# Attention preparation in four pieces of two PSUM banks, and a changed order of late work, in a two-layer attention and expert kernel

## The chip, the cores and the metric

The kernel runs on one core of a Trainium2 chip. The metric is device time of one execution in microseconds (us), the median of the runs shown. Five engines work from queues of their own: PE (matrix products), DVE (vector work), ACT (activation functions and copies), POOL (general work) and SP, which here only issues DMAs. Each works through its queue in the order in which the program was written, and an instruction at the head of a queue that waits holds everything behind it. The kernel schedules by hand: the order in the Python text is the order on the engines.

## The reference

The input x is 32 x 128 x 256, that is 4096 tokens of 256 channels in fp32.

```python
# layer 0: attention over all 4096 tokens, 8 heads of 32, causal in t = position % 128
x1 = (h - mu) / sqrt(var + 1e-5) * ln_g + ln_b
q  = (x1 @ wq.T + bq + sym_emb) @ wQ.T + bQ          # two products, folded into one matrix
K, V = h @ wK.T + bK, h @ wV.T + bV
attn = softmax(where(mask, -inf, Q K^T / sqrt(32)));  ctx = attn V
x = h + alpha * (ctx @ out_w.T + out_b)
# layer 1: windowed attention (24 wide), then a dense mixture of 8 experts
t = t + window_attention(ln(t))
w = softmax(ln(t) @ Wr + br)                          # per token, 8 shares
t = t + sum_e w_e * (relu(bn(relu(bn(ln(t) W1_e)) W2_e)) Wo_e + bo_e)
```

## The kernel before

**Layer 0.** The queries are cut into 8 blocks of 512 (`b`), the heads into 2 groups of 4 (`g`). A unit `(b, g)` is a row of steps (`k`), one for each 128 keys that the block may see; a block has 8b+5 steps (6 for b=0), 265 in all. One step is: `scores` (L1299), four heads' score products side by side on the PE, one head into tile `sa` (a pool of one bank), three heads into `sb` (a tile of three banks, from the pool `ps_b` that holds two such tiles); `product` (L1389), the attention-times-V products `av` of the step two before; `exps`, the ACT exponentials of `sa` (L1312) and `sb` (L1314) into one of five `pt` buffers; and `add`, which on DVE adds the `pt` of the step before to the running sum `acc` (L1375, two instructions of 128x1024). On a step that crosses the mask, POOL writes zeros into `pt` (L1326) before anybody reads it. At the end of a unit, ACT copies `av` out between its two exponentials (L1404), the PE sums `acc` over keys (L1419), ACT copies that out (L1447), and SP, DVE and DMA invert and spread it; six and twelve steps later follow `invert` and `scale` (L1471).

Between steps, the loop takes pieces of work from a generator, at an even rate of `count` pieces in a block. `prep(b + 1)` makes the next block's operands in seven pieces: the transposes of x (`pst`, L984), K for the two groups (`psk`, L993), V in two halves (`psv`, L1027), Q for the two groups (`psq`, L1006). Each piece takes a `sb` tile from `ps_b`, uses one bank of it (the transposes two), and gives it back when ACT (K, V) or DVE (Q: a multiplication L1010, then an addition L1014) has read it. So the second step after a piece waits with its three `sb` heads for that reader. Q's readers stand in DVE's queue behind the `add` of the step before. Two more generators follow in blocks 2 and 3: `output_weights` (load, transposes `ps_wo` L1053, copies L1059 and alpha on DVE, then `ps_ob`) and `expert_norms`.

In block 1 the layer-norm statistics of the last tokens are ready, and the roots for blocks 2 to 7 are made at once after that step's piece (`rstd_block(2, NBLK)`: an addition on DVE, a root on ACT, a reciprocal on DVE); the root needs another ACT table than the exponentials. `send_rstd` (L972, L976) then writes the reciprocals to DRAM and reads them back spread over partitions, as `rb`, which Q's multiplication needs.

In block 7 the tokens of the first four blocks are loaded, and on POOL the output bias is added to the first 12 tiles of 128 tokens (`with_bias`, L904; `FIRST` is 12).

**Layer 1.** 64 rounds (`work`: 8 token blocks x 8 experts) of two expert layers, each layer in two halves `first` and `last` of the seven products of a fast 2x2 scheme (`Layer`, L2017), and the weighted output products (`combine`, L2074). Everything else (projection of the next tokens, window attention, routing, biases) is a list of `jobs` with costs and predecessors. `insert` puts up to three jobs at a time between the halves; a job is taken when the planner's clock `now` is `LATER` = 3.2 planner units beyond each predecessor and the share allowed by the block's due times is not used up. Within `last`, ACT makes three `relu`s, of which two wait for a DVE addition (L2059).

Of the kernel before, what the change touches and what calls it, by code (L numbers as in the profile page):

```python
# [823 lines left out]
def fast_kernel(ctx: ExitStack, tc: tile.TileContext, ins: dict, out: bass.AP, narrow):  # L824
# [101 lines left out]
    with ExitStack() as l0:  # L926
# [63 lines left out]

        def project_k(b, g, hT, ps):
            for c in range(2):
                nc.tensor.matmul(  # L993
                    ps, lhsT=wKT[:, c, g * P : (g + 1) * P], rhs=hT[:, c, :],
                    start=(c == 0), stop=(c == 1),
                )
            nc.scalar.activation(
                kT[:, g, b * BLK : (b + 1) * BLK], ps, AF.Identity, bias=colT[:, g, 5:6]
            )

        def project_q(b, g, hT, ps, wait=False):
            if b not in qblk:
                qblk[b] = px.tile([P, NGRP, BLK], F32, tag="q", name=f"q{b}")
            q = qblk[b]
            for c in range(2):
                nc.tensor.matmul(  # L1006
                    ps, lhsT=wcT[:, c, g * P : (g + 1) * P], rhs=hT[:, c, :],
                    start=(c == 0), stop=(c == 1),
                )
            nc.vector.tensor_tensor(q[:, g, :], ps, rblk[b], op=ALU.mult)  # L1010
            qv = q[:, g, :].rearrange("p (t n) -> p t n", n=N)

            def biases():
                nc.vector.tensor_tensor(  # L1014
                    qv, qv, cq[:, g, :].unsqueeze(1).to_broadcast([P, BLK // N, N]), op=ALU.add
                )

            if wait:
                return biases
            biases()  # L1020

        def project_v(b, i2, hT, ps):
            ps = ps.rearrange("p (k d) -> p k d", d=D)
            for k in range(2):
                i = 2 * i2 + k
                for c in range(2):
                    nc.tensor.matmul(  # L1027
                        ps[:, k, :], lhsT=hT[:, c, i * P : (i + 1) * P], rhs=wVT[:, c, :],
                        start=(c == 0), stop=(c == 1),
                    )  # L1030
            j = b * TPB + 2 * i2
            nc.scalar.copy(v[:, j : j + 2, :], ps)

        def prep(b, banks):

            hT = transposed_x(b, banks(f"pst{b}", 2))
            yield
            for g in range(NGRP):
                project_k(b, g, hT, banks(f"psk{b}_{g}", 1)[0])
                yield  # L1040
            for i2 in range(TPB // 2):
                project_v(b, i2, hT, banks(f"psv{b}_{i2}", 1)[0])
                yield
            for g in range(NGRP):
                project_q(b, g, hT, banks(f"psq{b}_{g}", 1)[0])
                yield

# [129 lines left out]
        def output_weights(banks):  # L1177
# [7 lines left out]
            yield  # L1185
            transposed(woT, wo_n, "ps_wo", banks, False)
            nc.vector.tensor_scalar(woT, woT, alpha, None, op0=ALU.mult)
# [51 lines left out]
        with ExitStack() as at:  # L1239
# [267 lines left out]
            load_at = {2: ("xs", 5, 6), 3: ("xs", 7), 5: ("xg", 2), 7: ("xg", 3)}  # L1507

            def rest_of_first():
                for i2 in range(TPB // 2):  # L1510
                    project_v(0, i2, hT0, banks(f"psv0_{i2}", 1)[0])
                    yield
                for g in range(1, NGRP):
                    project_k(0, g, hT0, banks(f"psk0_{g}", 1)[0])
                    yield
                    project_q(0, g, hT0, banks(f"psq0_{g}", 1)[0])
                    yield

            todo, done, count = iter(()), 0, 0
            later = {}  # L1520
            for n in range(len(steps) + LAG + 1 + 16):
                if n < len(steps):
                    b, g, k = steps[n]
                    own = sum(len(units[b, i]) for i in range(NGRP))
                    if g == 0 and k == 0:
                        for _ in todo:
                            pass
                        todo, done, count = iter(()), 0, 7
                        if b + 1 < NBLK:
                            todo = prep(b + 1, banks)  # L1530
                            if not b:
                                send_rstd(1)
                        if b == 0:
                            todo, count = itertools.chain(rest_of_first(), todo), 11
                        if b == 2:
                            todo, count = itertools.chain(todo, output_weights(banks)), 10
                        if b == 3:
                            todo, count = itertools.chain(todo, expert_norms(banks)), 9
                        if 2 <= b < NBLK - 2:
                            xblk[b + 2] = load_x(b + 2, "xg")  # L1540
                    scores(b, g, k)
# [23 lines left out]
                if n < len(steps):  # L1565
                    at_step = g * len(units[b, 0]) + k + 1
                    closing = any(f is close_sums for f, _ in later.get(n, []))
                    while done < count * at_step // own and not (closing and b):
                        next(todo, None)
                        done += 1  # L1570
                    if b == NBLK - 1 and not g and k < 4:
                        load_tokens(
                            k, tok.tile([P, TPB, D], F32, tag="xg", name=f"tokens{k}")
                        )
                    if n in load_at:
                        for lb in load_at[n][1:]:
                            got = xstat if load_at[n][0] == "xs" else xblk
                            got[lb] = load_x(lb, load_at[n][0])
                    for sb_, si in stat_at.get(n, ()):
                        stats(sb_, si, xstat[sb_])  # L1580
                        if (sb_, si) == (NBLK - 1, TPB - 1):
                            rstd_block(2, NBLK)
                            send_rstd(2)
                            nsq = px.tile([P, NTILE], F32, tag="nsq", name="nsq", bufs=1)
                            nc.gpsimd.tensor_tensor(
                                nsq, mean0[:, :, 0], mean0[:, :, 0], op=ALU.mult
                            )
                            nc.gpsimd.tensor_tensor(nsq, nsq, mean0[:, :, 1], op=ALU.add)
                            nc.vector.tensor_reduce(hmax, nsq, axis=AX.X, op=ALU.max)
                    if 1 < b < NBLK - 1 and not g and k == 1:  # L1590
                        send_rstd(b + 1)
                    if b == NBLK - 1 and g and 4 <= k < 4 + FIRST:
                        with_bias(k - 4)
                for f, u in later.pop(n, []):
# [409 lines left out]
    class Layer:  # L2004
# [43 lines left out]
        def last(self):  # L2048
            x, t, w, s, out = self.x, self.t, self.w, self.s, self.out
            if t is None:  # L2050
                self.plain(1)
                return
            self.product(self.a[:, 0], w[:, 1, :P], x[:, 1, :HB], False)
# [7 lines left out]
                self.u.unsqueeze(1).to_broadcast([P, 2, HB]), op=ALU.add,  # L2061
            )
            relu(out[:, 0, HB:], out[:, 0, HB:], self.l, e, 0)
            relu(out[:, 1, :], out[:, 1, :], self.l, e, 1)
# [273 lines left out]
    for b in range(1, NBLK):  # L2338
# [33 lines left out]
        for r2 in range(TPB // 2):  # L2372
# [3 lines left out]
            )  # L2376
        job(("sums", b), 0, lambda b=b: expert_sums(b), ("xfT", b, 0), ("xfT", b, 1))
        job(("route", b), 0.55, lambda b=b: route(b), ("xfT", b, 0), ("xfT", b, 1))
        job(("routet", b), 0.15, lambda b=b: turn_route(b), ("route", b))
        job(("routex", b), 0, lambda b=b: route_exponentials(b), ("routet", b))  # L2380
        job(("routed", b), 0, lambda b=b: route_shares(b), ("routex", b))
        job(("turn_shares", b), 0.2, lambda b=b: turn_shares(b), ("routed", b))
        for r2 in range(TPB // 2):
            job(
                ("bias", b, r2), 0.6, lambda b=b, r2=r2: output_biases(b, r2),
                ("turn_shares", b),
            )
# [26 lines left out]
    now, spent = 0.0, 0.0  # L2414
    LATER = 3.2
    SPAN = E * 9.5
# [24 lines left out]
    def insert(passed):  # L2441
# [4 lines left out]
        while k < len(jobs) and few < 3:  # L2446
            name, cost, f, needs = jobs[k]
            if cost and spent >= allowed():
                k += 1
                continue  # L2450
            if all(done_at.get(q, now) + LATER <= now for q in needs if q in known):
                f()
# [20 lines left out]
    for k in range(len(work)):  # L2473
# [7 lines left out]
        if k + 1 < len(work):  # L2481
# [5 lines left out]
            if not k:  # L2487

                one.last()
            else:  # L2490
                insert(1.73)
        if k >= 2:
            combine_half()
# [4 lines left out]
        if one and k:  # L2498
            one.last()
            insert(1.3)  # L2500
# [3 lines left out]
        if one:  # L2504
            name = f"th{k + 1}"
            h1[k + 1] = one.out, token_sums(one.out, "th", name) if k + 1 >= PLAIN else None
        two.last()
        h2[k] = two.out
        insert(1.3)
    while halves:  # L2510
        combine_half()
# [47 lines left out]
```

## Time and profile before

| what | value |
| --- | --- |
| median of three runs | 1516.95 us (1516.86 to 1518.46) |
| the profiled execution: its own time, its span | 1517.62 us, 1515.8 us |
| busy: PE, DVE, ACT, POOL | 1472.3, 1205.0, 941.3, 166.6 us |
| layer 0, from the first exponential to the end of its scores | 20 to 717 us of the span |
| expert rounds of layer 1 | about 790 to 1506 us |
| mean granted PE clock | 0.995 of full speed |

Spans and busy times are of the one profiled execution. A busy engine isn't an engine at its peak: matrix products that wait for one of their operands part of the time can count as busy. So a stretch is read by the pace of its steps, that is by the distance of the starts of successive exponentials, and not only by busy shares. A wait in the profile is put down to the engine that came last.

### The profile page before, as it was taken

The numbers are of one execution on the slowest core, as the hardware profiler recorded it, in microseconds if no ns is written. First come the engines' busy times: TensorE is split into PE (matmuls) and PEld (weight loads), VectorE is DVE, ScalarE is ACT, GpSimd is POOL, SyncE is SP. The second block draws the span as 40 slices with busy tenths as digits, with TensorE's granted clock in tenths as the row PEclk, the third lists the DMA queues.
The fourth block names the chain that finished last, engine by engine and source line by source line (L and its number), as shares of the span: only waits on it lengthen the run. The fifth ranks groups of instructions, "written<-read, shape, count | busy, mean of one in ns | idle before, by whom it ended". The sixth has DMA issues, their size and how long they took to land.

```text
span 1515.8 us, 23636 instructions
## 1 busy us (share of the span) xinstructions
PE 1472.3 (97%) x8873; PEld 843.4 (56%) x8873; DVE 1205.0 (79%) x2191; ACT 941.3 (62%) x1356; POOL 166.6 (11%) x318
## 2 busy tenths in 40 slices
PE   9999999999999999999899999999999999999998
PEld 5333232222322222222558787887888788788887
DVE  5678789899989898999647777777787777777775
ACT  4777778878878888987353544554355444544443
POOL 2101011100000000071153012100011000000000
PEclk9999999999999999999999999999999999999999
DMA  7120101010000010000333333433333334333342
GB/s 150 26 51 19 36 1 37 2 29 9 3 13 8 1 50 22 1 9 10 108 119 104 105 119 108 135 123 107 118 108 122 104 116 141 106 121 118 126 153 65
DMA packets 96377, 110.15 MB, mean 73 GB/s; under 512 B 17949, under 2 KB 85232, under 8 KB 96256
## 3 DMA queue, kind: packets, MB, share of 16 engines
q1 hardware_dynamic: 93280, 106.87, 23.7%
q8 instruction: 72, 1.18, 0.3%
q0 software_dynamic: 1888, 0.91, 0.3%
q10 hardware_dynamic: 1088, 0.79, 0.2%
q14 instruction: 49, 0.40, 0.1%
HBM read 98.87 MB, written 8.53 MB: 71 GB/s over the span
## 4 chain that ended last, share of the span: by engine, by line
PE 70%; DVE 17%; ACT 6%; issue 5%; DMA 0%; POOL 0%; ACTq 0%; DVEq 0%; POOLq 0%
PE psh L2017 18%; PE sa L1299 13%; PE av L1389 12%; PE psy L2074 11%; DVE acc L1375 6%; ACT h L2000 3%; PE psk L993 2%; PE psv L1027 2%; PE psq L1006 2%; PE sb L1299 2%; PE psk L1766 2%; DVE h L2059 1%; PE sums L1419 1%; ACT pt L1314 1%; DVE tokens L2082 1%
## 5 line engine op out<-in xcount | busy, mean ns | idle before, releaser
L1375 DVE TENSOR_TENSOR acc<-acc,pt 128x1024 f32<-128x1024 f32 (+2 forms) x470 | 523.8, 1178 | 35.7 <-POOL pt L1326 20.9
L1314 ACT ACTIVATE pt<-sb 128x1536 f32<-128x1536 f32 (+1 forms) x265 | 382.8, 1445 | 6.2 <-PE sb L1299 6.1
L1299 PE MATMUL sa<-q,kT 32*128 32x512 f32 (+3 forms) x576 | 297.5, 602 | 8.7 <-ACT pt L1312 5.4
L1299 PE MATMUL sb<-q,kT 32*128 32x512 f32 (+3 forms) x1728 | 301.2, 603 | 3.2 <-DVE woT L1059 1.6
L2000 ACT ACTIVATE h<-h,bshift,bscale 128x256 f32<-128x256 f32 x244 | 159.2, 699 | 222.2 <-DVE h L2059 222.1
L1389 PE MATMUL av<-pt,v 128*32 128x512 f32 (+3 forms) x2304 | 283.1, 571 | 0.5
L2074 PE MATMUL psy<-wo,h 128*128 128x256 f32 x1024 | 242.8, 380 | 0.0
L2074 PEld LDWEIGHTS psy<-wo,h 128*128 128x128 f32 x1024 | 191.8, 190 | 29.1 <-issue 2.9
L1312 ACT ACTIVATE pt<-sa 128x512 f32<-128x512 f32 (+1 forms) x265 | 157.9, 596 | 80.5 <-PE sb L1299 44.2
L1299 PEld LDWEIGHTS sa<-q,kT 32*128 32x128 f32 x576 | 86.3, 184 | 212.6 <-ACT pt L1312 164.3
L1389 PEld LDWEIGHTS av<-pt,v 128*32 128x32 f32 x2304 | 47.9, 108 | 199.4 <-issue 175.0
L2082 DVE SCALAR_TENSOR_TENSOR tokens<-psy,w,tokens 128x256 f32<-128x256 f32 x256 | 111.1, 475 | 35.2 <-PE psy L2074 34.9
L2044 DVE TENSOR_TENSOR u<-psh,u 128x256 f32<-128x256 f32 x122 | 51.2, 419 | 104.8 <-ACT u L2043 104.5
L1326 POOL MEMSET pt<- 32x256 f32 (+4 forms) x123 | 52.1, 424 | 609.3 <-ACT pt L1314 521.9
L2000 ACT ACTIVATE h<-psh,bshift,bscale 128x256 f32<-128x256 f32 (+1 forms) x132 | 75.6, 574 | 46.7 <-PE psh L2017 39.1
L1299 PEld LDWEIGHTS sb<-q,kT 32*128 32x128 f32 x1728 | 90.5, 184 | 14.0 <-ACT pt L1314 6.5
L2043 ACT COPY u<-psh 128x256 f32<-128x256 f32 x122 | 43.9, 360 | 80.3 <-PE psh L2017 79.9
L2017 PE MATMUL psh<-tx,s 128*128 128x256 f32 x366 | 89.9, 382 | 0.3 <-DVE tx L1990 0.3
L2017 PE MATMUL psh<-th,s 128*128 128x256 f32 x366 | 90.2, 383 | 0.0
L2059 DVE TENSOR_TENSOR h<-psh,u 128x512 f32<-128x512 f32 x122 | 83.2, 682 | 4.5 <-PE psh L2017 4.5
L2017 PEld LDWEIGHTS psh<-th,s 128*128 128x128 f32 x366 | 70.3, 192 | 9.9 <-DVE h L2059 0.2
L2017 PEld LDWEIGHTS psh<-tx,s 128*128 128x128 f32 x366 | 69.8, 191 | 10.4 <-DVE tx L1990 0.7
(335 smaller groups left out, 1788.2 us busy)
## 6 DMA issues: line engine op xcount, KB each, us to landing
w<-in_L_ffn_W_dram SPq DMA_DIRECT2D x128, 256.0 KB
s<-kept SPq DMA_DIRECT2D x56, 512.0 KB
wo<-in_L_ffn_Wo_dram SPq DMA_DIRECT2D x64, 256.0 KB
xg<-in_x_dram SPq DMA_DIRECT2D x32, 128.0 KB
tokens<-in_x_dram SPq DMA_DIRECT2D x8, 512.0 KB
kept<-s SPq DMA_DIRECT2D x8, 512.0 KB
out_dram<-tokens SPq DMA_DIRECT2D x32, 128.0 KB
rec<-flat SPq DMA_DIRECT2D x60, 64.0 KB
```

Source lines behind the costliest of these rows:

```text
L1299: nc.tensor.matmul((sb[:, h - 1, :] if h else sa)[:, at : at + w], lhsT=kT[rows, gg, j * P : (j + 1) * P], rhs=q[rows, gg, lo : lo + w], s ...
L1312: nc.scalar.activation(pt[:, 0, used], sa[:, used], AF.Exp, scale=SCALE)
L1314: nc.scalar.activation(pt[:, 1:, used], sb[:, :, used], AF.Exp, scale=SCALE)
L1326: nc.gpsimd.memset(rows, 0.0)
L1375: nc.vector.tensor_tensor(acc[:, hs, cols], acc[:, hs, cols], pt[:, hs, at : at + w], op=ALU.add,)
L1389: nc.tensor.matmul(av[h * HD : (h + 1) * HD, lo : lo + w], lhsT=v[:, j, (g * HG + h) * HD : (g * HG + h + 1) * HD], rhs=pt[:, h, at : at + w],
L2000: nc.scalar.activation(dst, src, AF.Relu, bias=bshift[:, m, k : k + 1], scale=bscale[:, m, k : k + 1])
L2017: nc.tensor.matmul(ps, lhsT=w, rhs=x, start=start, stop=True, skip_group_check=True)
L2044: nc.vector.tensor_tensor(u, a[:, 1], u, op=ALU.add)
L2059: nc.vector.tensor_tensor(flat.rearrange("p (k c) -> p k c", k=2), self.q, self.u.unsqueeze(1).to_broadcast([P, 2, HB]), op=ALU.add,)
L2074: nc.tensor.matmul(ps[:, i, :], lhsT=ht[:, c, r * P : (r + 1) * P], rhs=wo[k][:, c, :], start=(c == 0), stop=(c == 1),)
L2082: nc.vector.scalar_tensor_tensor(out=tokens(n), in0=ps[:, i, :], scalar=w[:, r, e : e + 1], in1=tokens(n), op0=ALU.mult, op1=ALU.add,)
```

## The change

1. `prep` has four pieces: the transposes, both groups of K, both halves of V, both groups of Q. Each of the last three uses two banks of one `ps_b` tile, all its products first and then the two copies (for Q: multiplication and addition of group 0, then of group 1). The rest of block 0's own preparation is done likewise in two pieces. `count` is 5 (8 in blocks 0 and 2, 7 in block 3).
2. `output_weights` takes one tile with two banks for its transposes, and ACT copies them.
3. After the last statistics, only a mark is set. Ahead of the next piece the addition, the root and a reload of the exponentials' table are put in (`root_rstd`), and one step later the reciprocal, `send_rstd(2)` and the rest (`invert_rstd`).
4. The tokens of blocks 0 to 2 are loaded in block 5, those of block 3 in block 6; the 12 `with_bias` run as six in block 5 and six in block 6.
5. In layer 1, `expert_sums` stands behind `route` and `turn_route` in the list; the second half of `output_biases` of a block waits for the first; `LATER` becomes a variable, 3.2 for rounds 0 to 7 and 4.7 from round 8; the two late `relu`s of the second expert layer are issued after the `insert` that follows.

```diff
         def prep(b, banks):
             hT = transposed_x(b, banks(f"pst{b}", 2))
             yield
-            for g in range(NGRP):
-                project_k(b, g, hT, banks(f"psk{b}_{g}", 1)[0])
-                yield
...
+            pss = banks(f"psk{b}", 2)
+            keys = [project_k(b, g, hT, pss[g], True) for g in range(NGRP)]
+            for f in keys:
+                f()
+            yield
...
+            pss = banks(f"psq{b}", 2)
+            queries = [project_q(b, g, hT, pss[g], later=True) for g in range(NGRP)]
+            for f in queries:
+                f()
+            yield
...
-            transposed(woT, wo_n, "ps_wo", banks, False)
+            pss = banks("ps_wo", 2)
...
+            for c in range(2):
+                nc.scalar.copy(woT[:, c, :], pss[c][:, :D])
...
+            def root_rstd():
+                cols = slice(2 * TPB, NTILE)
+                nc.vector.tensor_scalar(
+                    rstd0[:, cols], mean0[:, cols, 1], 1e-5, None, op0=ALU.add
+                )
+                nc.scalar.activation(rstd0[:, cols], rstd0[:, cols], AF.Sqrt)
+                ready(AF.Exp)
+
+            def invert_rstd():
+                cols = slice(2 * TPB, NTILE)
+                nc.vector.reciprocal(rstd0[:, cols], rstd0[:, cols])
+                send_rstd(2)
...
+            u, z = NBLK - 3, NBLK - 2
+            tokens_at = [(u, 0, 2), (u, 0, 4), (u, 1, 0), (z, 1, 0)]
...
-                        todo, done, count = iter(()), 0, 7
+                        todo, done, count = iter(()), 0, 5
...
+                    if due == 2:
+                        invert_rstd()
+                        due = 0
                     while done < count * at_step // own and not (closing and b):
+                        if due == 1:
+                            root_rstd()
+                            due = 2
                         next(todo, None)
                         done += 1
...
-                    if b == NBLK - 1 and g and 4 <= k < 4 + FIRST:
-                        with_bias(k - 4)
+                    if NBLK - 3 <= b < NBLK - 1 and g and 4 <= k < 4 + FIRST // 2:
+                        with_bias((b - NBLK + 3) * FIRST // 2 + k - 4)
...
-        job(("sums", b), 0, lambda b=b: expert_sums(b), ("xfT", b, 0), ("xfT", b, 1))
         job(("route", b), 0.55, lambda b=b: route(b), ("xfT", b, 0), ("xfT", b, 1))
         job(("routet", b), 0.15, lambda b=b: turn_route(b), ("route", b))
+        job(("sums", b), 0, lambda b=b: expert_sums(b), ("xfT", b, 0), ("xfT", b, 1))
...
-                ("turn_shares", b),
+                ("turn_shares", b), *([("bias", b, r2 - 1)] if r2 else []),
...
+        if k == E:
+            later = 4.7
...
-        two.last()
+        relus = two.last()
         h2[k] = two.out
+
         insert(1.3)
+        relus()
```

## The prediction

> **What bounds the kernel now.** I read the page first, then the steps of layer 0 in the timeline, then the waits of the PE.
>
> ```profile
> PE 1472.3 (97%) x8873; PEld 843.4 (56%) x8873; DVE 1205.0 (79%) x2191; ACT 941.3 (62%) x1356; POOL 166.6 (11%) x318
> PE 70%; DVE 17%; ACT 6%; issue 5%; DMA 0%; POOL 0%; ACTq 0%; DVEq 0%; POOLq 0%
> L1375 DVE TENSOR_TENSOR acc<-acc,pt 128x1024 f32<-128x1024 f32 (+2 forms) x470 | 523.8, 1178 | 35.7 <-POOL pt L1326 20.9 <-ACT pt L1314 12.7
> ```
>
> The PE bounds the span, but 17% of the chain that ended last is DVE, nearly all of it `acc` in layer 0. A plain step there takes 2.07 us: score products began at 440.48 and 442.55, and 1.06 + 1.0 us of PE work fill it. ACT needs 0.60 + 1.45 = 2.05. DVE needs more: twenty-one adds took 23.93 us near the end, so one per 1.136 us and 2.27 us a step. DVE falls 0.20 us behind in every plain step and catches up only while the PE does a preparation piece (`psq` 1.91 us). Five `pt` buffers let it fall back by about 6 us (the exponential of step n+5 would start 8.3 us after that of step n ends; the add takes 2.3); then steps take 2.27. Where DVE's backlog meets something that needs DVE at once, the PE loses. Block 5:
>
> ```profile
> 428.85 1.98 PE L1006 MATMUL psq<-hT,wcT 128*128 128x512 f32 x4
> 432.83 1.12 PE L1299 MATMUL sa<-q,kT 32*128 32x512 f32 x2
> 434.02 0.67 DVE L1010 TENSOR_TENSOR q<-psq,rb 128x512 f32<-128x512 f32 x1
> 434.74 1.13 PE L1299 MATMUL sb<-q,kT 32*128 32x512 f32 x6 [0.79 <-DVE q L1010]
> 439.58 0.60 ACT L1312 ACTIVATE pt<-sa 128x512 f32<-128x512 f32 x1 [2.20 <-PE sb L1299]
> ```
>
> Q's products ran at 428.85; DVE read them only at 434.02, after its adds; `sb` of the second next step needs that tile and began at 434.74 instead of with `sa` at 432.83. Exponentials started at 433.99, 439.58 for consecutive `sa` of steps 17 and 18: with the delayed `sb` this pair of steps took 3.5 us more than 2 x 2.07. Two other places, and block 7:
>
> ```profile
> 64.10 1.28 ACT L915 ACT_TABLE_LOAD   x1
> 65.63 1.28 ACT L1312 ACT_TABLE_LOAD   x1
> 154.75 0.75 DVE L1059 COPY woT<-ps_wo 128x256 f32<-128x256 f32 x2
> 155.22 1.44 PE L1299 MATMUL sb<-q,kT 32*128 32x512 f32 x6 [1.57 <-DVE woT L1059]
> 646.17 25.15 POOL L904 TENSOR_TENSOR tokens<-tokens,outb 128x256 f32<-128x256 f32 x11
> 655.63 13.43 DVE L1375 TENSOR_TENSOR acc<-acc,pt 128x1024 f32<-128x1024 f32 x8 [0.64 <-ACT pt L1314]
> ```
>
> Two table loads in front of exponentials; `woT` as Q above; and eight adds in 13.43 us while POOL adds biases, a pitch of 1.67 instead of 1.136. In block 7 DVE is busy without a gap from 655.63 to the end of its adds at 719.8 and so sets the end of layer 0. In layer 1 the PE's named waits between 790 and 1506 us sum to 12.8 us:
>
> ```profile
> PE psa L1831 <- ACT ptl L1822: 2.1, 2, 1.2
> PE ptf L1895 <- DVE xf L1885: 1.7, 2, 0.9
> PE psa L1831 <- DVE tokens L1959: 1.4, 1, 1.4
> PE psp L1819 <- ACT s L1808: 1.4, 1, 1.4
> PE psrt L1920 <- DVE lgT L1915: 1.2, 1, 1.2
> ```
>
> These are jobs whose predecessor on ACT or DVE wasn't done, each under 1.5 us.
>
> **What the Trainium skill says.** "SBUF — State Buffer", Who interferes with whom: a DVE instruction with two SBUF inputs contends with a POOL instruction that reads SBUF, and the second is held up. The trace agrees in kind (adds of 1.22 us take 1.75 beside `with_bias`, and the first bias lasted 9.41 us, until DVE had a gap), though both go on at a lower rate. "ScalarE: Activation LUTs", What ACT_TABLE_LOAD costs: 1283 ns, with a drain beside it; here the two loads are 1.28 us each and the whole episode (64.10 to 66.93) 2.83, so no further drain is seen. The same lines give the price used below.
>
> **The change part by part.**
>
> *Biases out of block 7.* Ten adds in the second half of block 7 were slowed by 1.67 - 1.136 = 0.53 us, 5.3 us, and a later one by 0.45. DVE sets the end there, so -5.6 us. In blocks 5 and 6 they cost DVE at most 12 x 0.53 = 6.4 us. What hides it: DVE is idle there for 8.0 of 114.9 and 8.9 of 127.2 us, POOL can start them only in a DVE gap, and these are at the boundary of the two units and at the V piece just after it. I take 0; without this cover it is +6.4. The three early 512 KB token loads precede reciprocal DMAs on SP, which have five or more steps to spare; nothing.
>
> *Pieces of two banks.* PE, ACT and DVE work is the same: 7 pieces of 1.0 + 6 x 1.91 = 12.5 us a block become 1.0 + 3 x 3.83. K's and V's copies (0.69, 0.58 each) end 0.7 us after the piece; the tile is needed 2.07 after it: no wait. Q: DVE reads group 0, adds its bias, reads group 1: 0.69 x 3 = 2.07 us after it is through with its earlier add, and the tile is needed 3.83 + 2.07 after the piece starts. So there is no loss while DVE is through with that add within 3.83 us of the piece's start; one bank alone allows 1.91 + 2.07 - 0.69 = 3.3. The add ends 1.3 us plus the backlog after the start, so the backlog may be 2.5 rather than 2.0. Losses of this kind before, from the starts of exponentials against steps without such a piece: 3.5 (block 5), 2.0, 1.25 and 3 x 0.4 at block starts (second Q piece as last step of the block: 5.05, 4.29, 3.4 against 3.04), 0.6 and 0.95 in blocks 4 and 6: 9.5 us. Afterwards, by the order of the changed program, Q stands 3 to 11 steps behind V, where DVE has just had 3.8 us to catch up. Backlog at Q: 7 to 9 steps x 0.20 + 0.24 (`invert`) + 0.3 (mask step) = 2.0 to 2.4 in blocks 4 and 5, no loss; 10 steps, and `scale` (1.26) before it, 3.85 in block 6: 1.3 us of wait and some 0.7 since `sa` then runs without `sb`. With 1 us for the rest, 3.0. So -6.5; bounds -9.5 and +3. The last steps of a unit, where the PE had also waited for Q, are relieved, and nothing else stands there.
>
> *Roots.* Before, step 10 came 6.42 us after its predecessor, with a K piece 3.98 expected: 2.4 lost. Afterwards 2 x 1.28 + 0.4 us of ACT work stand beside K's 3.83 us of PE, but K's two copies (1.38) follow them, so the next exponential is about 0.7 late. -1.7. `rb` is due later: the write of 4-byte elements took from 65.98 until the read could issue at 75.14, and SP must first wait for another reciprocal; I get a landing near 85 us and Q's read near 86. If late, +2; so 0 to -2.4.
>
> *Output weights.* Steps 38 and 39 took 6.04 and 3.82; 2 x 2.07 and 1.3 us of PE work leave 4.4 lost. One tile and ACT copies take this away, but now the transposes come one step behind the load instead of three: the load issues behind four DMAs that wait for the unit's sums (in the trace 139.57 to 142.08), and needs 3 to 4 us; the PE arrives about 2.6 us early. With 0.6 for `ps_ob`, -1.2 (0 to -4).
>
> *Block 0.* K now follows the transposes at once and waits for two copies (1.2 us); shorter turns of tiles give as much back: 0.
>
> *Layer 1.* Waiting 1.5 units longer covers waits up to 1.5 us. Of the PE gaps between rounds 8 and 63, about 8.5 us are of this kind; the bias order frees banks (the 1.4 of `psa` on `tokens`); `relu`s behind the jobs' ACT work free ACT, which sat 222 us before them, and their reader comes more than 5 us later. Chains get longer (some 19 links), yet in the changed program each block's transposed tokens stand at least 20 us of expert products before their first use. I take -7, bounds -12 and +2.
>
> Sum: -5.6 - 6.5 - 1.7 - 1.2 - 7 = -22.0. The profiled execution, 1517.6 (span 1515.8), goes to 1495.6; its time is 0.7 above the median, so the median goes from 1516.95 to 1495.
>
> **The rivals.**
> (a) Layer 1 gives nothing: new waits come at other jobs. For: jobs move, and with them their bank turns. Against: every wait in the list is shorter than what is added. 1502.
> (b) Layer 0 gives half: `rb` or `wo_n` late, the biases meeting Q in blocks 5 and 6 (+6.4 on backlogs that stand near the limit). 1503.
> (c) Slower: DVE is at its full backlog of 6 us at every Q piece. It then reads Q 7.3 us after the start, 3.5 too late, with 1.1 for the heads apart: 4.6 x 7 blocks = 32 us, against 25 of gain without the 3 above: 1524. It decides from a mean loss of 3.6 a block, a backlog of 5. Against: V's 3.8 us just before it.
> (d) The moved work was hidden anyway: 1517. Against it stand the gap-free DVE of block 7 and the named waits.
> (e) Layer 1 gives all 12 and Q loses nothing: 1487.
>
> **How the numbers follow.** Chances: forecast 0.62 (1489 to 1501), (a) 0.14, (b) 0.13, (e) 0.04, (c) 0.04, (d) 0.03. A measurement of this kernel can tell about 0.2%, 3 us. The range 1485 to 1507 holds all but (c), (d) and the rims of the others. Faster 0.93, same 0.03, slower 0.04.
>
> **What would show it.** Right: steps of block 7's second half at 2.07 until near its end and adds of 1.22 us; no `sb` waiting for `q` but in block 6; no table load between exponentials of block 1 except beside K; layer 0's scores ending about 15 us earlier; PE waits after round 8 under 3 us. Wrong: adds of 1.75 us followed by `sb` waiting for `q` in blocks 5 and 6; `ps_wo` waiting more than 3 us for its load; DVE waiting for `rb`; new waits of `psa`, `ptf` or `psy` in layer 1.

## The result, and the profile after

The changed kernel takes 1493.32 us (median of four runs, 1492.53 to 1494.66) against 1516.9 of the kernel before, run beside it (four runs, 1515.5 to 1518.46). The ratio is 0.9845, 95% interval 0.9828 to 0.9862: 23.6 us faster, where 22.0 were forecast. The profiled execution took 1492.53 us, its span 1490.7.

These lines are from the page of the changed kernel: busy times, the chain that ended last, and the group of DVE's adds.

```profile
PE 1457.9 (98%) x8873; PEld 842.3 (56%) x8873; DVE 1201.1 (81%) x2189; ACT 936.5 (63%) x1357; POOL 159.5 (11%) x318
PE 83%; DVE 9%; ACT 4%; issue 2%; DMA 1%; POOL 1%; SPq 0%; ACTq 0%; DVEq 0%; POOLq 0%
L1406 DVE TENSOR_TENSOR acc<-acc,pt 128x1024 f32<-128x1024 f32 (+2 forms) x470 | 518.1, 1168 | 31.5 <-POOL pt L1357 16.2
```

DVE's share of the chain falls from 17% to 9%, and 1% is now DMA and 1% POOL, which had none. The prediction took the 17% of before as nearly all `acc` in layer 0. That reading was wrong: by the page's list of the chain by line `acc` (L1375) has 6%, and of the 17% about 10 lie behind 720 us, in layer 1. Three places that the prediction showed, in the timeline of the changed kernel: the roots in block 1, Q in block 5, and the end of block 7 (start, duration, engine, line, output and inputs, and in brackets the wait before it and what ended it).

```profile
65.84 1.28 ACT L1545 ACT_TABLE_LOAD   x1
69.18 0.22 ACT L1545 ACTIVATE rstd<-rstd 128x24 f32<-128x24 f32 x1 [2.06 <-DVE rstd L1542]
69.42 1.28 ACT L911 ACT_TABLE_LOAD   x1
...
424.54 3.70 PE L1012 MATMUL psq<-hT,wcT 128*128 128x512 f32 x8
428.28 0.69 DVE L1018 TENSOR_TENSOR q<-psq,rb 128x512 f32<-128x512 f32 x1 [0.40 <-PE psq L1012]
429.33 0.60 ACT L1343 ACTIVATE pt<-sa 128x512 f32<-128x512 f32 x1 [3.75 <-PE sb L1330]
...
677.75 28.86 DVE L1406 TENSOR_TENSOR acc<-acc,pt 128x1024 f32<-128x1024 f32 x26
```

At Q, DVE now waits for the PE (0.40 us) and not the PE for DVE. In block 7 the adds stand at one per 1.11 us (28.86 / 26). But between the two table loads ACT waits 2.06 us for an addition on DVE.

The two lists below have the PE's waits in the changed kernel, the longest in layer 0 and then all between 790 and 1484 us, in layer 1 (total us, times, longest):

```profile
PE sa L1330 <- ACT pt L1343: 3.6, 4, 2.0
PE ps_ob L1225 <- DVE bvb L1222: 3.0, 1, 3.0
PE av L1420 <- POOL pt L1357: 2.6, 1, 2.6
PE ps_wo L1213 <- DMA wo_n<-in_L_conv_out_w_dram: 2.0, 1, 2.0
```

```profile
PE psh L2076 <- DVE h L2105: 1.2, 4, 0.4
```

The second list is complete. The prediction gave 12.8 us as the sum of such waits before; the same list of the kernel before sums to 14.0. Of these, 1.3 are two waits of `ptx` at 795 and 796 us which the changed kernel still has, at 786 and 787 us, just ahead of the list. So like for like 12.7 fell to 1.2. The first list has three waits that the kernel before did not have. So the sum came out near the forecast, but not from where it was forecast. The table has the distance between the first exponentials of successive blocks, and from the last exponential of layer 0 to the end of the span.

| us | before | after | difference | forecast of it |
| --- | --- | --- | --- | --- |
| blocks 0, 1 | 31.3, 45.3 | 30.8, 44.7 | -0.5, -0.6 | 0, -2.1 |
| block 2 | 66.5 | 69.7 | **+3.2** | -1.6 |
| block 3 | 76.5 | 80.7 | **+4.3** | 0 |
| blocks 4, 5, 6 | 95.2, 114.8, 127.3 | 92.7, 109.4, 128.3 | -2.5, -5.4, +1.0 | together -5 to -6 |
| block 7, to its last exponential | 136.1 | 129.2 | -6.8 | -6.8 |
| layer 0 | | | -7.3 | -15 |
| the rest, to the end | 802.8 | 785.2 | **-17.6** | -7 |

(The forecast by block follows from the prediction's list of losses, as far as that names blocks. The last exponential of layer 0 starts at 713.1 us before and at 705.6 after.) Layer 0 gave half of what was forecast, as in rival (b), and layer 1 more than the most that was thought possible.

These PE and DVE lines of the changed kernel show what goes wrong in block 2:

```profile
145.57 0.63 PE L1213 MATMUL ps_wo<-ident,wo_n 128*128 128x128 f32 x4 [1.97 <-DMA wo_n<-in_L_conv_out_w_dram]
151.70 5.02 DVE L1406 TENSOR_TENSOR acc<-acc,pt 128x768 f32<-128x768 f32 x5 [2.03 <-POOL pt L1357]
156.64 0.36 DVE L1222 COPY bvb<-colT 128x128 f32<-128x128 f32 x2
157.00 2.04 PE L1225 MATMUL ps_ob<-woT,bvb 128*128 128x256 f32 x4 [3.01 <-DVE bvb L1222]
158.98 1.22 PE L1330 MATMUL sa<-q,kT 32*128 32x512 f32 x1
```

`bvb` is a constant spread over 128 columns, two small copies. They stand in DVE's queue behind the adds, and with the pieces moved `ps_ob` comes right after the step on the mask, where DVE had first waited 2.03 us for POOL's zeros and then had five adds to do. And these are POOL and PE in block 3:

```profile
222.66 7.25 POOL L1246 TENSOR_SCALAR bandb<-bandb,abias 128x160 f32<-128x160 f32 x1 [12.82 <-DMA abias<-in_L_attn_bias_dram]
230.56 1.63 POOL L1357 MEMSET pt<- 32x256 f32 x3
232.25 1.93 PE L1420 MATMUL av<-pt,v 128*32 128x384 f32 x16 [2.61 <-POOL pt L1357]
```

With four pieces instead of seven in front of it, `expert_norms` begins at step (3, 1, 5) instead of (3, 1, 10), and POOL's work for `bandb` (waiting 12.82 us for its load) lands ahead of the zeros of step (3, 1, 7) instead of behind them. In the kernel before, the zeros of that step waited for ACT alone, and POOL's work for `bandb` began at 226.79 us, behind them:

```profile
225.11 1.63 POOL L1326 MEMSET pt<- 32x256 f32 x3 [20.24 <-ACT pt L1314]
```

After each of these waits the PE runs at half speed for a while: `ps_ob` takes 2.04 us for four matmuls that take 1.13 in the run with both mends below, the `sa` after it 1.22 instead of 0.69, the 16 products of `av` 1.93 instead of 1.07. The records of the granted clock have 0.5 for 3.41 us from 146.5 and from 156.7 and for 6.83 us from 231.8. The kernel before had four such stretches of 3.41 us before the end, at 155.9, 435.8, 780.6 and 1060.5; the last three, at Q in block 5, in the prologue of layer 1 and in its rounds, are gone in this profile.

### The profile page after: what moved, and what is told of

Read it like the earlier page. It is cut to its first block, busy times and chain, and to the rows that moved or that the text cites. A ratio compares the mean times of both kernels' runs of the same rounds, so it can differ in the third digit from the quotient of the medians.

```text
span 1490.7 us, 23636 instructions
## 1 busy us (share of the span) xinstructions
PE 1457.9 (98%) x8873; PEld 842.3 (56%) x8873; DVE 1201.1 (81%) x2189; ACT 936.5 (63%) x1357; POOL 159.5 (11%) x318
## 4 chain that ended last, share of the span: by engine, by line
PE 83%; DVE 9%; ACT 4%; issue 2%; DMA 1%; POOL 1%; SPq 0%; ACTq 0%; DVEq 0%; POOLq 0%
PE psh L2076 22%; PE sa L1330 15%; PE av L1420 15%; PE psy L2137 13%; DVE acc L1406 2%; PE psv L1039 2%; PE psq L1012 2%; PE psk L1825 2%; PE psk L993 2%; PE sums L1450 1%; ACT h L2059 1%; PE sb L1330 1%; PE psh L2081 1%; PE pso L1515 1%; PE pss L1837 1%
## 5 line engine op out<-in xcount | busy, mean ns | idle before, releaser
L1406 DVE TENSOR_TENSOR acc<-acc,pt 128x1024 f32<-128x1024 f32 (+2 forms) x470 | 518.1, 1168 | 31.5 <-POOL pt L1357 16.2
L2076 PEld LDWEIGHTS psh<-th,s 128*128 128x128 f32 x366 | 69.5, 190 | 9.5
```

Of the source, the lines that this page charges most:

```text
L1406: nc.vector.tensor_tensor(acc[:, hs, cols], acc[:, hs, cols], pt[:, hs, at : at + w], op=ALU.add,)
L2076: nc.tensor.matmul(ps, lhsT=w, rhs=x, start=start, stop=True, skip_group_check=True)
```

## The experiments

Each median is of four runs. The kernel before, run beside them in three groups, had medians of 1517.73, 1516.96 and 1517.34 us. The 1493.32 of the changed kernel is from the group of the result. The medians of before differ by 0.8 us, so a difference of less than about 1 us between a run here and the changed kernel means nothing.

**Half the change at a time.** One run has only those parts of the diff that are in layer 0, another only those in layer 1.

> Layer 0's parts of the change alone, layer 1 as before. Theory (new waits in blocks 2 and 3 of layer 0, each followed by some 3.4 us at half the PE clock, take back about 8 of what the pieces, roots and biases give): 8 to 9 us faster than before, 1508.5; blocks 2 and 3 last about 69.7 and 80.7 us as in the changed kernel, 3 to 4 more each than before. Rival 1 (layer 0 is worth the predicted 15, and the late end of its scores in the changed kernel comes from layer 1's code or from this one profile): 1502, with blocks 2 and 3 no longer than before. Rival 2 (the halves act together: 25 us is not the sum): far from 1508.5, and with the run of layer 1 alone a sum other than 24.

> Layer 1's parts of the change alone (bank of waiting time 4.7 from round 8, order of sums, order of biases, late relus), layer 0 as before. Theory (every wait of a job between rounds 8 and 63 goes, and with them two stretches of half PE clock): 15 to 16 us faster, 1501.5; PE gaps above 0.12 us between 790 us and the end fall from 20 to about 6 us. Rival (layer 1 is worth the predicted 7, the rest of its gain in the changed kernel comes from layer 0's handing over earlier): 1510, with some 13 us of such gaps left.

Layer 0 alone takes 1509.21 us (ratio 0.9951, 0.9934 to 0.9968), 8.5 less than before; blocks 2 and 3 last 68.8 and 79.8. Layer 1 alone takes 1501.59 (0.9894, 0.9874 to 0.9914), 16.1 less; the PE's named waits from 775 us on fall from 14.9 to 3.5 us, and no stretch of half clock is left there before the last microseconds. The sum, 24.6, is the 23.6 of the whole within what is measured: no action of the halves on each other is seen, and the forecast's split of 15 and 7 is refuted.

**Block 2.** This is the changed kernel with the output weights loaded at the block's start and `bvb` filled one piece earlier.

```diff
+            bvb = px.tile([P, 2, P], F32, tag="bvb", name="bvb", bufs=1)
+            for c in range(2):
+                nc.vector.tensor_copy(bvb[:, c, :], colT[:, c, 6:7].to_broadcast([P, P]))
             pss = banks("ps_wo", 2)
...
-            bvb = px.tile([P, 2, P], F32, tag="bvb", name="bvb", bufs=1)
-            for c in range(2):
-                nc.vector.tensor_copy(bvb[:, c, :], colT[:, c, 6:7].to_broadcast([P, P]))
...
-                            todo, count = itertools.chain(todo, output_weights(banks)), 8
+                            ow = output_weights(banks)
+                            todo, count = itertools.chain(todo, iter([None]), ow), 8
...
+                        if b == 2:
+                            next(ow)
```

> The changed kernel, but the load of the output weights is issued at the start of block 2 and the two copies that fill bvb stand on DVE with the piece of ps_wo, seven steps ahead of ps_ob. Theory (the wait of ps_wo for its load, 2.0, and of ps_ob for bvb, 3.0, each cost their own length and some 1.2 to 1.7 us more of work at half clock): 6 to 8 us faster than the changed kernel, about 1486.5; block 2 lasts 62 to 64 us instead of 69.7, and no matmul of it runs at half clock. If the waits cost only their own length: 5 us, 1488.5. Rival (the PE would have waited for DVE's backlog anyway, since DVE is the slowest in these steps): 0 to 2 us, 1492, with the time back in waits for pt.

The run took 1486.98 us, 6.3 less than the changed kernel. Block 2 lasts 62.96 instead of 69.73: 6.8 us for waits of 1.97 + 3.01 = 4.98. That the other 1.8 are the half clock behind the waits is likely, not shown. Of six other runs that keep both waits, two also have two stretches of half clock in this block; it lasts 69.5 there, with waits of 4.6. The other four have one stretch, and the block lasts 68.8 to 69.0 with waits of 5.6 to 5.7, so that only 0.3 is left over.

**Block 3.** The loads and POOL's work of `window` get places of their own.

```diff
+            yield
             nc.gpsimd.memset(bandb, 0.0)
...
+                    if (b, g, k) == (3, 0, 4):
+                        norm_loads()
+                    if (b, g, k) == (3, 1, 8):
+                        next(win, None)
```

(`win` is `window()`, now a generator; `norm_loads` advances it to its `yield` and issues the loads of `bn`.)

> The changed kernel, but the loads of expert_norms and window() are issued in step (3, 0, 4) and POOL's part of window() in step (3, 1, 8), after the memset of the mask step (3, 1, 7) instead of ahead of it; the transposes psbn stay where they are. Theory (the memset behind bandb cost the PE 2.6 us of wait and then some 6.8 us at half clock): 4.5 to 6 us faster than the changed kernel, about 1488; block 3 lasts 75 to 76 us instead of 80.7. If only the wait counts: 2.6 us, 1490.7. Rival (block 3 is longer because of its pieces, not of the memset): no change, 1493.

The run took 1488.91 us, 4.4 less than the changed kernel. Block 3 lasts 77.0 instead of 80.7, 3.7 for a wait of 2.61; 75 to 76 were expected. In the six other runs that keep this wait (2.60) the block lasts 79.8, with one stretch of half clock of 3.41 us and not of 6.83, and there only 0.1 is left over beyond the wait. POOL's lines in the mended run are:

```profile
226.78 1.63 POOL L1361 MEMSET pt<- 32x256 f32 x3 [19.41 <-ACT pt L1349]
230.74 1.00 POOL L1247 TENSOR_SCALAR bandb<-bandb,abias 128x160 f32<-128x160 f32 x1
```

The zeros wait for ACT alone. The instruction that took 7.25 us takes 1.00 here, with DVE adding in both cases. In the changed kernel it ended at 229.91, 0.6 us after an unbroken row of DVE's adds did; here it ran in the middle of such a row. Why, isn't settled.

**Both mends together.**

> The changed kernel with both mends: output weights loaded at the start of block 2 and bvb filled with the piece of ps_wo; loads of expert_norms in step (3, 0, 4), POOL's part of window() in step (3, 1, 8). Theory (the two waits are separate, each with its own stretch of half clock): their gains add, 6.3 and 4.4 off 1493.3, so 1482.6; blocks 2 and 3 last about 63 and 77 us. Rival (the time goes to DVE's backlog, which is the same for both): the second mend gives less than half, 1485 or more.

The run took 1482.64 us (0.9778, 0.9759 to 0.9797), 10.7 less than the changed kernel, with blocks 2 and 3 at 62.97 and 77.01: the gains of 6.3 and 4.4 add. In the profile no stretch of half clock is left before the last microseconds, and the two products of block 2 wait for nobody:

```profile
144.14 0.65 PE L1216 MATMUL ps_wo<-ident,wo_n 128*128 128x128 f32 x4
151.43 1.13 PE L1225 MATMUL ps_ob<-woT,bvb 128*128 128x256 f32 x4
```

**The biases back in block 7.** The token loads go back with them.

```diff
-            tokens_at = [(u, 0, 2), (u, 0, 4), (u, 1, 0), (z, 1, 0)]
+            tokens_at = [(NBLK - 1, 0, k) for k in range(4)]
...
-                    if NBLK - 3 <= b < NBLK - 1 and g and 4 <= k < 4 + FIRST // 2:
-                        with_bias((b - NBLK + 3) * FIRST // 2 + k - 4)
+                    if b == NBLK - 1 and g and 4 <= k < 4 + FIRST:
+                        with_bias(k - 4)
```

> The changed kernel with the token loads and the twelve with_bias back in block 7. Theory (the biases hold DVE up where it sets the end of layer 0, and cost nothing in blocks 5 and 6): 5.6 to 6.8 us slower than the changed kernel, about 1499.5; block 7 lasts 136 instead of 129.2 us, blocks 5 and 6 stay within 0.5 of 109.4 and 128.3. Rival 1 (the biases do cost DVE in blocks 5 and 6, and some of the 6.8 is only moved): blocks 5 and 6 together 2 to 6 us shorter, total 1495 to 1497. Rival 2 (block 7 got shorter by its pieces of Q and K, not by the biases): no change, 1493.

The run took 1496.69 us, 3.4 more than the changed kernel and less than expected. In the profile block 7 lasts 135.1 instead of 129.2, with a stretch of half clock at 687.5 us in it, block 5 lasts the same, and block 6 0.9 less: 4.9 net, so a small part of the gain is only moved. This profiled execution took 1497.93 us and has block 1 at 46.27 instead of 44.68, which the edit does not touch (more on this below). The four executions lie in two pairs, at 1495.2 to 1495.5 and at 1497.9 to 1498.0, so the worth of this part is known only roughly: 2 to 5 us.

**Parts of layer 1 undone, one at a time.** First, the planner's distance:

```diff
-            later = 4.7
+            later = 3.2
```

> The changed kernel with the planner's distance kept at 3.2 through all rounds. Theory (the longer distance is what took the job waits of layer 1 away, the order of jobs and the late relus being a small part): 7 to 11 us slower than the changed kernel, about 1502, with some 8 us of PE gaps above 0.12 us and one or two stretches of half clock back between 800 and 1480 us. Rival (the late relus and the orders do most of it): 0 to 4 us slower, 1495.

The run took 1498.39 us, 5.1 more than the changed kernel, less than the 7 to 11 expected. The PE's named waits after 790 us are 3.3 instead of 1.2 (`ptf` for `xf`, `psbo` for `wT`, `psh` for `h`). The profile also has a stretch of half clock at 772.6; it stands ahead of round 8, where the edit begins to act, so a part of the 5.1 may not be the edit's. Next, the late relus:

```diff
-        insert(1.3)
-        relus()
+        relus()
+        insert(1.3)
```

> The changed kernel with the two late relus of the second expert layer issued ahead of the jobs again. Theory (waits of the expert products for DVE's u and h, whose inputs these relus and the jobs' ACT work share, were about 4 us in the kernel before): 2 to 4 us slower, 1496. Rival 1 (the relus had 5 us to spare and their place means nothing): 0 to 1 us, 1493.5. Rival 2 (relus last hold their reader up, so issuing them early helps): 1 to 2 us faster.

The run took 1498.16 us, 4.8 more, where 2 to 4 were expected (its profile, too, has a stretch at 771.7, ahead of the rounds). The named waits are 5.2 instead of 1.2. ACT and PE in the profile of this run show how:

```profile
842.69 1.30 ACT L2059 ACTIVATE h<-h,bshift,bscale 128x256 f32<-128x256 f32 x2 [2.11 <-DVE h L2118]
843.90 0.35 ACT L1881 COPY ptl<-psp 128x256 f32<-128x256 f32 x1
844.30 1.13 PE L1890 MATMUL psa<-xl,ptl 128*128 128x256 f32 x4 [1.24 <-ACT ptl L1881]
```

This is the same place in the changed kernel:

```profile
839.63 0.35 ACT L1881 COPY ptl<-psp 128x256 f32<-128x256 f32 x1
841.84 1.30 ACT L2059 ACTIVATE h<-h,bshift,bscale 128x256 f32<-128x256 f32 x2 [1.34 <-DVE h L2118]
```

The two relus at the head of ACT's queue wait for DVE, and the copy `ptl` of a job, whose products `psp` were done at 839.6, waits behind them until 843.9; with the relus last it runs in that gap. Last, the order of the jobs (`sums` ahead of `route` again, second half of the biases free of the first):

> The changed kernel with the job of the expert sums ahead of route again and without the order between the two halves of a block's biases. Theory (the order frees the banks for which psa waited 1.6 us for the tokens, with a stretch of half clock behind it): 2 to 4 us slower than the changed kernel, 1496. Rival (with the longer distance of 4.7 the waits are covered anyway): within 1 us, 1493.

The run took 1496.72 us, 3.4 more. Its profile has one long wait in layer 1, followed by 6.8 us at half clock:

```profile
PE psy L2137 <- DVE tokens L2018: 3.3, 1, 3.3
```

It is a wait for the bias halves, but another than the one expected (`psa` for the tokens). What the order of `sums` is worth alone is not known, since the edit undoes both. The three undone singly give 5.1 + 4.8 + 3.4 = 13.3 of the 15.9 us that lie between layer 0 alone and the whole change. That they cover for each other in the rest is possible, not shown.

**Pieces of one bank in the mended kernel.** Here `prep` is as before (seven pieces, counts 7, 9, 10, 9), and all else as in the kernel with both mends.

> The kernel with both mends, but with the next block's operands prepared in seven pieces of one bank again; roots, biases, output weights and layer 1 as changed. Theory (as predicted: pieces of two banks spare the waits for Q, 6.5 us): 6.5 us slower than the kernel with both mends, 1489, in blocks 4 (95.2 for 92.7), 5 (113 to 115 for 109.4) and 2 or 7 (1 to 2 more), block 3 about the same. Rival 1 (the shorter blocks come from the other parts): 1482.6. Rival 2 (smaller pieces are the better ones once no wait is left): below 1481.

The run took 1488.89 us, 6.25 more than with pieces of two banks: blocks 4 to 7 last 95.2, 113.3, 128.6 and 130.1 for 92.7, 109.4, 128.3 and 129.3; block 2 is 1.1 shorter, block 3 0.6 longer. Most of the loss is at Q, as forecast: the second step after the first Q piece lasts 2.62, 4.02 and 3.34 us in blocks 4 to 6 instead of 2.07, and the second step after the other Q piece, at the start of blocks 5 to 7, 4.86, 3.90 and 4.10 instead of about 3.28. That is 6.8 us, against 1.2 in the kernel with both mends (block 6 alone).

**The addition of the roots one step earlier.** This edit stands on top of both mends.

```diff
                             due = 1
+                            shift_rstd()
```

(`shift_rstd` is the `tensor_scalar` on DVE, taken out of `root_rstd`.)

> The kernel with both mends, and the addition on DVE that the roots of block 1 need issued with the last statistics, ahead of two adds, instead of with the root. Theory (in the changed kernel ACT waited 2.06 us for this addition behind DVE's adds, the next step came 8.06 after its predecessor, of which about 2 are lost, and in some executions a stretch of half clock follows): step 12 comes 6 us after its predecessor, block 1 lasts 42.6 instead of 44.7 us, total 1480.6, or 1479.5 if the half clock is gone too. Rival (ACT's two table loads and K's two copies set this step, not the addition): block 1 within 0.5 of 44.7, total 1482.6.

The run took 1479.96 us (1479.8 to 1480.17; ratio to the kernel before 0.9753, 0.9737 to 0.9769), 13.4 less than the changed kernel: this is the version that beats both. Step 12, counted from 0 over layer 0, comes 6.03 us after its predecessor instead of 8.08, and block 1 lasts 42.62. The root follows its table load at once:

```profile
66.19 1.28 ACT L1552 ACT_TABLE_LOAD   x1
67.49 0.22 ACT L1552 ACTIVATE rstd<-rstd 128x24 f32<-128x24 f32 x1
```

**What a wait costs beyond its length.** This comes from the profiles of the runs above. In block 1 of the changed code the PE waits 2.0 us for ACT. In every run with that code the block has one of two lengths. All but the last of a profile's clock records are multiples of 3.41 us long, and they start on a grid of that width, whose place differs from run to run. The second column is the share that the PE's records leave empty in the emptiest window of that grid within the block.

| run | window empty | block 1, us | clock in the next window |
| --- | --- | --- | --- |
| after | 36% | 44.68 | full |
| layer 0 alone | 46% | 44.67 | full |
| block 3 mended | 46% | 44.69 | full |
| relus first | 34% | 44.66 | full |
| both mends | 34% | 44.67 | full |
| block 2 mended | 59% | 46.32 | half |
| biases in block 7 | 60% | 46.27 | half |
| distance 3.2 | 56% | 46.23 | half |
| order undone | 60% | 46.27 | half |

The same wait costs 1.6 us more when one window holds most of it than when two share it. Two of these runs show it window by window (the window, its length, the busy time of PE, PEld, DVE, ACT and POOL with the number of instructions, the granted clock, the DMA share and GB/s). With block 2 mended, the emptiest window and the next:

```profile
70.65:74.06 3.41, 1.39 (x14) 0.47 (x16) 1.05 (x2) 3.40 (x7) 0.03 (x1) 1.00 0.13 20
74.06:77.47 3.41, 3.41 (x13) 1.73 (x6) 1.12 (x3) 1.75 (x2) 2.01 (x5) 0.50 0.06 5
```

With block 3 mended:

```profile
70.96:74.37 3.41, 1.85 (x16) 0.47 (x16) 0.57 (x2) 3.41 (x6) 0.46 (x2) 1.00 0.08 2
74.37:77.78 3.41, 3.41 (x19) 2.83 (x16) 1.59 (x5) 1.27 (x1) 1.58 (x4) 1.00 0.06 5
```

The two profiles with layer 0 as before (the kernel before, and layer 1 alone) agree: block 1 lasts 45.30 and 46.93, block 2 66.50 and 67.98, block 5 114.83 and 113.24, and each time the longer one has 3.41 us more of half clock, at a cost of 1.5 to 1.6 us. Over all 13 profiles, from 25 us after the start to 1440 us, 22 of 22 full-speed windows that were 56% empty or more were followed by half clock, and 3 of 8 between 50 and 55%. Eight windows below that were followed by it too, five of them at the start of layer 1 and three in the kernel before; what decides there stays open.

## Why the prediction was right in its sum and wrong in its parts

*Biases out of block 7* (-5.6): right for the block (5.8 to 6.8), while "I take 0" for blocks 5 and 6 holds for 5 and misses 0.9 in 6. By medians the part is worth 3.4, and 2 to 5 is what can be said.

*Pieces of two banks* (-6.5): right, 6.25 measured. The limit on DVE's backlog held too: no wait for Q in blocks 4 and 5 (DVE waited for the PE), and in block 6 a short one, with steps of 2.71 and 2.57 (by the exponentials of `sb`) instead of 2.07, 1.1 us where 1.3 + 0.7 were reckoned. Of the 9.5 us of losses before, though, 1.6 in block 5 were the clock's: there 3.5 were lost, and with the same pieces and no half clock behind them, 1.95.

*Roots* (-1.7, got -0.6): the step that failed is "2 x 1.28 + 0.4 us of ACT work stand beside K's 3.83 us". The root needs an addition on DVE, and DVE was two adds behind. I had counted ACT's instructions and not the one that they wait for. Without that wait the part gives 2.7 (block 1 falls from 45.3 to 42.6), more than forecast. `rb` in time was right.

*Output weights* (-1.2, got a loss): the load was priced well (2.6 early; 1.97 waited). The prediction gave `ps_ob` 0.6 and left out that `bvb` stands in DVE's queue behind the adds, next to a mask step: 3.01 us. With both out of the way the block gives 3.5 against before.

*Block 3* is missing from the sum. The change says nothing of `window`, but it moves it by five steps, and one engine's queue moves with it, POOL's, where the zeros of the mask are urgent. The order of the changed program shows it; the prediction followed the orders of PE, ACT and DVE for Q and that of SP for loads.

*Layer 1* (-7, bounds -12 and +2; got -16): the mechanism was right, the size not. The sum took 8.5 us of gaps as coverable, out of 12.7 of named waits, and left those for `u` and `h` (3.1) and others alone. Nearly all went (12.7 fell to 1.2, -11.4), and in this pair of profiles two half-clock stretches went with them; at 1.6 each, as in block 1, that is an estimate of 3.2, together 14.6 of the 16. Such stretches come and go between runs of the same layer 1: the run with block 2 mended has one in the prologue, at 767, and layer 0 alone, whose layer 1 is that of before, has one at 771 but none behind its wait of 1.44 us at 1050, where the kernel before has one. The relus were named as a help but got no number; they are worth 4.8. The misreading of DVE's 17% goes with this: about 10 of them were layer 1's, and in the changed kernel about 5 are.

*Nowhere priced*: that a wait of 2 to 3 us is followed by 3.4 us at half speed. "TensorE: Matmul & The Clock Gate", Part 1, of the Trainium skill has the free-running window of 3413 ns, and the clock's records agree (3.413 us and multiples); but it puts the fall to half after an idle window, and its section "HAM oscillation" names gaps of more than about 3.4 us. Here waits of 1.97 and 2.61 us were enough, when one window held most of them. The profile of before already showed it: behind the wait of 1.44 us at 1059 us six products of `psh` took 2.65 us, against 1.46 just ahead of it, and in block 5 3.5 us were lost around a wait listed with 0.79.

So two errors with opposite signs, about 7 us in layer 0 and 9 in layer 1, made a good sum, and that they met was luck. Rival (b), "layer 0 gives half", was true for layer 0. Of its causes only the late load of `wo_n` was there, with 1.97 us, and it was not the main one. The signs listed beforehand did their work: "layer 0's scores ending about 15 us earlier" failed (7.5), which is what led to blocks 2 and 3.

## What to carry to other kernels

When pieces of work are spread at an even rate, a change of their number moves everything behind them: list what each moved piece puts into every queue, the small constants and POOL's work too, and see what urgent instruction stands next behind it or before it. Issue what needs only old data (a load, a spread constant, one addition) long ahead of the piece that uses it. And price a PE wait of about 2 us or more at its length plus up to 1.7 us. This is an estimate: half of the 3.41 us that may follow at half clock. Block 1 gave 1.6 of it or nothing, by the place of the grid; in blocks 2 and 3 often only 0.1 to 0.3 was left over.

## What was not expected of the hardware

The half clock came after waits of 1.97 us, and once of 1.44, and went by a grid of 3.413 us: the same code has block 1 at 44.67 or 46.27 us, by the place of that grid. With all such waits mended the runs of a kernel also lie closer together (1479.8 to 1480.17, against 1492.53 to 1494.66); that this is the reason is likely, not shown.
